# Two graph-attention layers before a transformer layer: preparation placed among products, masks transposed as byte pairs, an order written out by hand

## The chip, the cores and the metric

The kernel runs on one NeuronCore of one Trainium2 chip. The core has five engines that run side by side and wait for each other through semaphores: TensorE (PE; its weight loads are shown as PEld), VectorE (DVE), ScalarE (ACT), GpSimd (POOL) and SyncE (SP), which here issues all DMA transfers from one queue in order. The metric is device time in microseconds (us) of one execution, lower is better.

## The reference

Three layers run one after the other on 4096 rows of 256 features and one 4096 x 4096 adjacency matrix of int32 (0 or 1). The first two are graph-attention layers with 8 heads of 32 features; the third is a transformer layer with masked attention.

```python
def _gat_layer(x, adj_mat, W, a):
    Wh = jnp.einsum('nd,hdo->hno', x, W)
    src = jnp.einsum('hno,ho->hn', Wh, a[:, :O])
    dst = jnp.einsum('hno,ho->hn', Wh, a[:, O:])
    e = jax.nn.leaky_relu(src[:, :, None] + dst[:, None, :], 0.2)
    e = jnp.where(adj_mat[None, :, :] > 0, e, NEG_INF)
    alpha = jax.nn.softmax(e, axis=-1)
    out = jnp.einsum('hnm,hmo->hno', alpha, Wh)
    return jnp.transpose(out, (1, 0, 2)).reshape(N, -1)

h   = elu(_gat_layer(x, adj, W1, a1)) + x
out = elu(_gat_layer(h, adj, W2, a2)) + h
# then: layer norm, masked attention with 8 heads (mask adj != 0), projection,
# layer norm, feed-forward of width 1024 with gelu, both with residuals
```

## The kernel before

**The algebra of a graph layer.** exp(leaky_relu(s + d)) is exp(s) exp(d) where s + d is positive and exp(0.2 s) exp(0.2 d) elsewhere. The kernel never forms the 4096 x 4096 scores. For each head it makes a 0/1 matrix of s >= -d, ANDs it with the mask, and multiplies it (as fp8 stationary operand) with values that have been multiplied with exp(d) and exp(0.2 d) beforehand. The f16 moving operand `vst` holds these values as a high and a low half, with a column for the softmax denominator. The masked sum of the second kind needs the mask itself as stationary operand.

**Blocks, pairs, groups.** A layer's rows are cut into blocks of tiles of 128 rows: layer 1 into 4, 4, 8, 8 and 8 tiles, layer 2 into four times 8 (`TILES`). For each block there are four pairs of heads, and for each pair 8 groups, one for 512 columns of the adjacency (four chunks `m` of 128). A group of eight tiles has 8 x 4 x 4 = 128 products (L1234): for each tile and chunk one of width 132, two of width 66 for the heads, and one of width 132 for the mask. The sums of a pair stand in six PSUM banks; in its last group they are evicted by ACT (L1240, L1246).

**Compare and AND.** `compare` makes the 0/1 matrices of a group two groups ahead: for each chunk and head a DVE comparison (L1023) or an ACT sign (L1021), then one DVE AND with the mask over 2048 int32 words (L1026). There are three such buffers (`t8`). The row terms s come as `s_b`, spread over the partitions by DMA from `s_d` in DRAM.

**Masks.** A mask unit loads 128 x 1024 int32 of the adjacency, clips them on DVE to bf16 (L844), turns eight 128 x 128 squares on PE (L849) and evicts 1024 columns to fp8 on ACT (L850). Block 0 uses its masks from SBUF; every mask is also stored to DRAM (`mask_d`), from where later blocks, layer 2 and the transformer layer fetch them. There are 128 units. Those of blocks 1 to 4 are spread over the groups of the block before.

**Preparation.** For each of 8 parts `q` of 512 rows: `features` transposes the rows (L916, evicted at L919), `term_rows` makes the row terms (L926, L934), and `values` for each of four tiles makes the values by two matmuls (L942), negates the d terms (L950), takes three small exps (L953, L961), the largest value (L954) for a check, scales (L962, L963), casts to the high half on ACT (L971) and subtracts for the low half on DVE (L972). Three of a layer's parts are prepared ahead of its first group, the others one per group beside the first five groups.

**Pair end.** `pair_end` puts four steps on a list, one of which is taken per group: load x, sum (L1053 to L1066), divide and exp (L1073 to L1079), and elu, residual and store (L1085 to L1088).

**Order.** In the graph layers a scheduler puts the instructions of each engine in order from the order of the program and from dependencies. The attention loop of the transformer layer has PE, ACT and DVE in program order (`manual_schedule`). The transformer layer projects q, k and v block by block (L1419, L1440), stores q and k as f16 halves to DRAM (`half_d`) and loads them back stacked (`stack`, L1387), with k's load right after its store; queries and masks of the first attention block are loaded after the last projection. Attention's rows are then projected and pass the feed-forward part (L1628 to L1673).

**Checks.** Conditions under which the fast method holds are gathered in the columns of one tile; if any is not met, `general_layers` computes everything again in a general way.

## Time and profile before

| what | value |
|---|---|
| median of 3 runs | 3524.0 us (3520.53 to 3526.98) |
| profiled execution | 3526.0 us, span 3524.0 us, clock 0.982 |
| PE busy | 3357.4 us (95%) |
| DVE busy | 2903.2 us (82%) |
| ACT busy | 2730.9 us (77%) |
| POOL busy | 1239.1 us (35%) |
| chain that ended last | PE 73%, DVE 11%, ACT 9%, DMA 3%, issue 2%, POOL 2% |
| graph layers | 0 to 1783 us |
| projections of q, k, v | 1796 to 1893 us |
| attention | 1914 to 3227 us |
| output part | 3239 to 3524 us |

The profile is one execution. Its page first gives busy time per engine, then 40 equal slices of the span with the busy share of each engine in tenths, then the chain of work that ended last. Groups of instructions follow, by line, engine and operation, with busy time, mean duration, and the idle time just before them with what ended it. A busy PE isn't a PE at its peak: matmuls are pipelined, and their ends are modelled. Idle time of an engine that isn't on the chain costs nothing.

### The profile page before, as it was taken

How to read it: one execution, taken by the hardware profiler on the slowest of the kernel's cores; microseconds unless marked ns; L12 is line 12 of the kernel's file. 1: busy time of each engine (PE TensorE's matmuls, PEld its weight loads, DVE VectorE, ACT ScalarE, POOL GpSimd, SP SyncE). 2: the span in 40 equal slices, each digit the busy share in tenths (PEclk: the TensorE clock that was granted, in tenths of full speed). 3: DMA queues.
4: the chain of work that ended last, by engine and by line, in shares of the span. 5: the costliest groups of instructions: out<-in, count | busy, mean ns of one | idle time of the engine just before them, and what ended most of it. 6: DMA issues, size and time to landing. Idle time of an engine off the chain costs nothing.

```text
span 3524.0 us, 99099 instructions
## 1 busy us (share of the span) xinstructions
PE 3357.4 (95%) x43715; PEld 2128.8 (60%) x43715; DVE 2903.2 (82%) x3580; ACT 2730.9 (77%) x3528; POOL 1239.1 (35%) x538
## 2 busy tenths in 40 slices
PE   6898999999989999999987999999999999997998
PEld 4698999999969999999963111111111121112666
DVE  5898999999889999999944999999999999996111
ACT  4799999998778888888854777777777777775332
POOL 0000000000000000000001999999999999996110
PEclk8999999999999999999998999999999999998999
DMA  4357554441221312111156010101010110002110
GB/s 140 123 191 242 167 167 157 157 123 39 68 62 33 86 39 80 45 58 37 26 135 171 10 40 13 37 19 31 25 25 25 25 37 13 28 9 68 44 47 25
DMA packets 199560, 252.76 MB, mean 72 GB/s; under 512 B 88080, under 2 KB 134672, under 8 KB 199120
## 3 DMA queue, kind: packets, MB, share of 16 engines
q1 hardware_dynamic: 199120, 246.34, 23.3%
q8 instruction: 344, 5.64, 0.7%
q14 instruction: 96, 0.79, 0.1%
HBM read 203.83 MB, written 42.47 MB: 70 GB/s over the span
## 4 chain that ended last, share of the span: by engine, by line
PE 73%; DVE 11%; ACT 9%; DMA 3%; issue 2%; POOL 2%; SPq 0%; DVEq 0%; ACTq 0%; POOLq 0%
PE bank L1234 34%; PE u_ps L1480 12%; PE u_av L1494 11%; PE u_dn L1494 6%; ACT t L1021 5%; DVE u_e L1489 4%; PE misc L1666 3%; PE misc L1419 2%; POOL u_both L1580 2%; DVE t L1023 1%; ACT u_ps L1487 1%; ACT stage L850 1%; DVE t L1026 1%; PE misc L1650 1%; PE turn L926 1%
## 5 line engine op out<-in xcount | busy, mean ns | idle before, releaser
L1234 PE MATMUL bank<-vst,t 128*128 128x66 f16 (+1 forms) x24576 | 1517.9, 203 | 22.0 <-DVE t L1026 15.5
L1234 PEld LDWEIGHTS <-t 128*128 128x128 fp8e4 x24576 | 1505.6, 97 | 33.2 <-DVE t L1026 18.0
L1234 PE MATMUL bank<-vst,mask 128*128 128x132 f16 x8192 | 1503.5, 222 | 0.0
L1021 ACT ACTIVATE t<-s_b,g_negd 128x1024 int8<-128x1024 f32 (+1 forms) x1296 | 1260.0, 1063 | 88.8 <-PE bank L1234 88.1
L1489 DVE SCALAR_TENSOR_TENSOR u_e<-u_mask,u_ps 128x1024 f32<-128x1024 uint8 x1024 | 1201.7, 1215 | 100.7 <-ACT u_ps L1487 95.8
L1580 POOL TENSOR_TENSOR u_both<-u_e 128x1024 f32<-128x1024 f32 x512 | 1199.8, 2367 | 238.5 <-DVE u_e L1489 238.3
L1487 ACT ACTIVATE u_ps<-u_ps 128x1024 f32<-128x1024 f32 x1024 | 1010.8, 1008 | 296.2 <-PE u_ps L1480 277.2
L1234 PEld LDWEIGHTS <-mask 128*128 128x128 fp8e4 x8192 | 803.6, 98 | 1.9 <-issue 0.9
L1026 DVE TENSOR_TENSOR t<-t,mask 128x2048 int32<-128x2048 int32 (+1 forms) x288 | 590.6, 2051 | 119.5 <-ACT t L1021 109.8
L1023 DVE TENSOR_SCALAR t<-s_b,g_negd 128x1024 fp8e4<-128x1024 f32 (+1 forms) x1008 | 638.5, 687 | 2.7 <-PE bank L1234 2.3
masks.py:197 POOL MEMSET u_ident<- 128x128 f32 x1 | 0.2, 204 | 1785.7 <-DMA u_wq<-in_L_gnn_w_qkv_dram 1785.7
L1480 PE MATMUL u_ps<-u_q,u_k 128*128 128x512 f16 x2048 | 580.5, 384 | 36.8 <-DMA u_q<-half_d 21.7
L1480 PEld LDWEIGHTS <-u_k 128*128 128x128 f16 x2048 | 139.2, 97 | 743.7 <-issue 685.4
L1494 PE MATMUL u_av<-u_e,u_v 128*32 128x512 f32 x4096 | 547.1, 605 | 0.0
L1494 PE MATMUL u_dn<-u_both,u_ones 128*32 128x512 f32 x2048 | 274.0, 605 | 1.3 <-POOL u_both L1580 1.3
L1494 PEld LDWEIGHTS u_av<-u_e,u_v 128*32 128x32 f32 x4096 | 80.9, 108 | 219.1 <-issue 211.3
L1657 ACT ACTIVATE u_hid<-misc,u_b 128x512 f32<-128x512 f32 x64 | 42.3, 683 | 142.9 <-PE misc L1650 142.8
L850 ACT ACTIVATE stage<-turn 128x1024 fp8e4<-128x1024 bf16 x112 | 114.2, 1037 | 1.1 <-PE turn L849 1.0
L1673 DVE TENSOR_TENSOR u_xres<-u_xres,misc 128x256 f32<-128x256 f32 x32 | 13.5, 421 | 122.7 <-PE misc L1666 122.7
L1666 PE MATMUL misc<-u_w,u_hid 128*128 128x256 f32 x512 | 111.8, 379 | 0.0
L1650 PE MATMUL misc<-ln_cols,u_w 128*128 128x512 f32 x256 | 111.2, 592 | 0.0
L1494 PEld LDWEIGHTS u_dn<-u_both,u_ones 128*32 128x32 f32 x2048 | 40.6, 108 | 110.9 <-issue 108.4
(104 smaller groups left out, 1749.8 us busy)
## 6 DMA issues: line engine op xcount, KB each, us to landing
g_rows<-in_adj_dram SPq DMA_DIRECT2D x128, 512.0 KB
mask<-mask SPq DMA_DIRECT2D x120, 256.0 KB
s_b<-s_d SPq DMA_DIRECT2D x56, 512.0 KB
u_mask<-mask SPq DMA_DIRECT2D x32, 512.0 KB
mask<-stage SPq DMA_DIRECT2D x28, 512.0 KB
half_d<-u_halves SPq DMA_DIRECT2D x32, 256.0 KB
u_k<-half_d SPq DMA_DIRECT2D x32, 256.0 KB
u_q<-half_d SPq DMA_DIRECT2D x32, 256.0 KB
```

The costliest lines, as they stand in the source:

```text
L850: nc.scalar.activation(staged[0].rearrange("p i g n -> p (i g) n")[:, :, t * P : (t + 1) * P], pt, AF.Identity, saturate=False,)
L1021: nc.scalar.activation(to.bitcast(I8), s, AF.Sign, bias=negd, scale=-1.0)
L1023: nc.vector.tensor_scalar(to, s, negd, None, op0=ALU.is_ge, saturate=False)
L1026: nc.vector.tensor_tensor(both, both, mask.unsqueeze(1).to_broadcast(list(both.shape)), op=ALU.bitwise_and)
L1234: nc.tensor.matmul(to, left, right, start=k not in opened, stop=last)
L1480: nc.tensor.matmul(ps[:, j, :], k_st[:, h, mt * P : (mt + 1) * P], q_st[:, h, :], start=True, stop=True,)
L1487: nc.scalar.activation(ps, ps, AF.Exp, scale=SCALE)
L1489: nc.vector.scalar_tensor_tensor(e, mask, 0.0, ps, op0=ALU.not_equal, op1=ALU.mult)
L1494: nc.tensor.matmul(to[j * O : (j + 1) * O, :], lefts[j], es[j // 2][:, j % 2, :], start=start, stop=stop,)
L1580: nc.gpsimd.tensor_tensor(both, es_of[i - 1][u], es_of[i][u], op=ALU.add)
L1650: nc.tensor.matmul(ph, w1_sb[:, k, f * P : (f + 1) * P], hn[:, k, :], start=(k == 0), stop=(k == DC - 1),)
L1666: nc.tensor.matmul(po[:, :D], hid[:, f, at : at + P], w2_sb[:, f, :], start=(f == 0), stop=(f == FC - 1),)
```

## The change

All of it lies in the graph layers and in the order of loads around them.

- Layer 1 has four blocks of 8 tiles like layer 2.
- A mask unit is now 256 adjacency rows by 512 columns. Two neighbouring rows are clipped into the two bytes of one 16-bit element (fp8), four 128 x 128 squares of f16 are transposed, and ACT copies 512 16-bit elements. A check sends four bit patterns through such a transpose.
- In `values`, the factor `UP` and the sign of the d terms are folded into the weights; one copy takes both kinds of terms out of PSUM; products are scaled with the exps directly. The cast and the subtraction for the low half become a later step (`split`), and the subtraction goes to POOL. The row terms are transposed from these copies (32 x 128) where two matmuls of 512 columns stood. The three checks on the largest values (`check_values`) are no longer called.
- `manual_schedule` now covers the graph layers: PE, ACT and DVE run in program order. `begin` prepares two parts and eight mask units; the other parts of layer 1 are prepared in groups 0 to 5, those of layer 2 in the last six groups of layer 1 and in groups 3 and 4 of layer 2. Each group has a list of steps with a place between 0 and 1, which are emitted after the tile that they fall on: preparation, compares for two groups on, the AND last, mask units and clips, pair-end steps.
- Pair ends have six steps; the exp has one of its own, two after the division. Sums stand in the eviction tile, the result in the tile of x.
- The next layer's weights reuse one tile and are loaded during block 1.
- In the transformer layer, `k_st` is allocated ahead of `v_sb`, k's stacked loads trail their stores by one block, the first queries and masks are loaded during the projections, and some pools are split; in the output part the projection weights are loaded first.

```diff
-TILES = ((4, 4, 8, 8, 8), (8, 8, 8, 8))
+TILES = ((8, 8, 8, 8), (8, 8, 8, 8))
...
-    mask_p = ctx.enter_context(tc.tile_pool(name="g_mask", bufs=11))
+    mask_p = ctx.enter_context(tc.tile_pool(name="g_mask", bufs=10))
-    rows_p = ctx.enter_context(tc.tile_pool(name="g_rows", bufs=3))
+    rows_p = ctx.enter_context(tc.tile_pool(name="g_rows", bufs=2))
...
+    def mask_load(nb, c, i):
+        r = rows_p.tile([P, 2, G * P], I32, name="g_adj", bufs=3)
+        at = STARTS[0][nb] * P + i * 2 * P
+        nc.sync.dma_start(
+            r,
+            adj[at : at + 2 * P, c * G * P : (c + 1) * G * P].rearrange("(k r) m -> k r m", r=2),
+        )
+        loaded[nb, c, i] = r
...
+    def mask_clip(nb, c, i):
+        v = rows_p.tile([P, G * P, 2], F8, name="adj_8", bufs=6)
+        nc.vector.tensor_scalar(
+            v.rearrange("p m r -> p r m"), loaded.pop((nb, c, i)), 1.0, -(2.0**-30),
+            op0=ALU.min, op1=ALU.max, saturate=False,
+        )
+        clipped[nb, c, i] = v.rearrange("p m r -> p (m r)").bitcast(F16)
+        load_ahead(1)
...
+    def mask_turn(nb, c, i):
+        if i == 0:
+            pool, name = (mask_p, "mask") if nb == 0 else (stage_p, "stage")
+            built[nb, c] = pool.tile([P, NW, G, HB], F8, name=name)
+            if nb == 0:
+                masks.setdefault((0, 0), []).append(built[nb, c])
+        v = clipped.pop((nb, c, i))
+        pt = turn_bank([P, G, P], F16)
+        for m in range(G):
+            nc.tensor.transpose(pt[:, m, :], v[:, m * P : (m + 1) * P], ident_h)
+        to = built[nb, c][:, i // 2].bitcast(U16)
+        nc.scalar.activation(to[:, :, i % 2 * P : (i % 2 + 1) * P], pt.bitcast(U16), AF.Copy)
...
+        def values(t):
+            at = G * q + t
+            pv = bank()
+            for c in range(DC):
+                nc.tensor.matmul(
+                    pv[:, : D + 2 * H],
+                    L.ft[q][:, c, t * P : (t + 1) * P],
+                    L.w_ext[:, c, :],
+                    start=(c == 0),
+                    stop=(c == DC - 1),
+                )
+            nc.vector.tensor_copy(
+                L.terms[:, :, at, :], pv[:, D : D + 2 * H].rearrange("p (k h) -> p k h", k=2)
+            )
+            big = some.tile([P, 2, H], F32, name="g_big")
+            for i, scale in enumerate((-1.0, -LRELU)):
+                nc.scalar.activation(big[:, i, :], L.negd[:, at, :], AF.Exp, scale=scale)
+            nc.scalar.activation(L.r[:, at, :], L.terms[:, 0, at, :], AF.Exp, scale=LRELU - 1.0)
+            nc.vector.tensor_reduce(
+                L.tops[:, at : at + 1], pv[:, :D], AX.X, ALU.max, apply_absolute_value=True
+            )
+            prod = held[t] = some.tile([P, H, 2, V1], F32, name="g_prod")
+            by_head = big.rearrange("p i h -> p h i").unsqueeze(3)
+            nc.vector.tensor_tensor(
+                prod[:, :, :, :O],
+                pv[:, :D].rearrange("p (h o) -> p h o", o=O).unsqueeze(2).to_broadcast([P, H, 2, O]),
+                by_head.to_broadcast([P, H, 2, O]),
+                op=ALU.mult,
+            )
+            nc.vector.tensor_scalar(prod[:, :, :, O:], by_head, UP, None, op0=ALU.mult)
+        def split(t):
+            part = held.pop(t).rearrange("p h i v -> p h (i v)")
+            halves = vst[q][:, t].rearrange("p h (k v) -> p h k v", k=2)
+            nc.scalar.copy(halves[:, :, 0, :], part)
+            nc.gpsimd.tensor_tensor(halves[:, :, 1, :], part, halves[:, :, 0, :], op=ALU.subtract)
+        def term_rows():
+            pr = bank()[: G * H, :P]
+            nc.tensor.transpose(
+                pr, L.terms[:, 0, G * q : G * (q + 1)].rearrange("p t h -> p (t h)"), ident_f
+            )
+            sr = some.tile([G * H, P], F32, name="g_sr")
+            nc.scalar.copy(sr, pr)
+            for t in range(G):
+                at = (G * q + t) * P
+                nc.sync.dma_start(s_d[l][:, at : at + P], sr[t * H : (t + 1) * H])
+        steps = [lambda c=c: features(c) for c in range(DC)]
+        for t in range(G):
+            steps.append(lambda t=t: values(t))
+            if t > 0:
+                steps.append(lambda t=t: split(t - 1))
+        return steps + [term_rows, lambda: split(G - 1)]
...
+        def step_wait():
+            pass
+        def step_exp():
+            nc.scalar.activation(held["ex"], held["z"], AF.Exp)
...
-        later.extend([step_load, step_sum, step_divide, step_out])
+        later.extend([step_load, step_sum, step_divide, step_wait, step_exp, step_out])
...
+    own = [(0, c, k) for c in range(NG) for k in range(2 * NW)]
+    for c in range(2, NG):
+        turns[c - 2] = own[2 * NW * c : 2 * NW * (c + 1)]
     for nb in range(1, len(TILES[0])):
+        units = [(nb, c, k) for c in range(NG) for k in range(2 * NW)]
+        since = max(NG - 2, (nb - 1) * per_block - 4)
+        until = nb * per_block - 4
         for u, unit in enumerate(units):
+            turns.setdefault(since + u * (until - since) // len(units), []).append(unit)
+    coming = own[: 2 * 2 * NW] + [u for i in sorted(turns) for u in turns[i]]
...
+    prepared = {i: (0, i + 2) for i in range(NG - 2)}
+    for l in range(1, NL):
+        start = l * len(TILES[0]) * per_block
+        for q in range(NG):
+            prepared[start + q + (-6 if q < NG - 2 else -3)] = (l, q)
...
+    def begin():
+        rows_ahead(0, 0)
+        weights_of(0)
+        load_ahead(3)
+        units = own[: 2 * 2 * NW]
+        for q in range(2):
+            for k, step in enumerate(preparation(0, q, spare_bank)):
+                step()
+                if q == 1 and k in (2, 4, 6, 8):
+                    mask_clip(*units[k // 2 - 1])
+        s_of[0, 0, 0] = s_fetch(0, 0, 0)
+        for k, u in enumerate(units):
+            mask_turn(*u)
+            if k + 4 < len(units):
+                mask_clip(*units[k + 4])
+            else:
+                mask_clip(*turns[0][k + 4 - len(units)])
+        for i in range(2):
+            for step in compare(i):
+                step()
...
+    ordered = {mybir.EngineType.PE, mybir.EngineType.Activation, mybir.EngineType.DVE}
+    ctx.enter_context(tc.manual_schedule(engines=ordered))
+    begin()
     for i, (l, nb, p, g) in enumerate(groups):
+        if l + 1 < NL and nb == 1 and p == 0 and g == NG - 1:
+            weights_of(l + 1)
+        fetches(i)
+        side = []
+        def beside(steps, since, until):
+            for k, step in enumerate(steps):
+                side.append((since + (until - since) * (k + 0.5) / len(steps), step))
+        made = prepared.get(i)
+        if i + 1 in prepared and prepared[i + 1][0] > 0:
+            if prepared[i + 1][1] in (0, NG - 2):
+                rows_ahead(*prepared[i + 1])
+        if made:
+            steps = preparation(*made, lambda: turn_bank([P, 512], F32))
+            beside(steps, 0.0, 0.9)
+        if i + 2 < len(groups):
+            steps = compare(i + 2)
+            beside(steps[:-1], 0.25 if made else 0.0, 0.95)
+            beside(steps[-1:], 0.96, 1.0)
+        beside([lambda u=u: mask_turn(*u) for u in turns.get(i, ())], 0.0, 0.9)
+        clips = turns.get(i + 2, ()) if i >= NG - 2 else turns.get(i + 1, ())
+        if i == NG - 2:
+            clips = turns.get(i + 1, []) + clips
+        beside([lambda u=u: mask_clip(*u) for u in clips], 0.1, 1.0)
+        beside([take] * (3 if l > 0 and nb == 0 and p == 0 else 1), 0.1, 1.0)
+        side.sort(key=lambda step: step[0])
...
-            if slots:
-                slots.pop(0)()
-        while slots:
-            slots.pop(0)()
+            while side and (n == tiles - 1 or side[0][0] * tiles < n + 1):
+                side.pop(0)[1]()
...
+                for b in (nb - 1,) if nb + 1 < NNB else (nb - 1, nb):
+                    if b >= 0:
+                        at = slice(b * NB, (b + 1) * NB)
+                        stack(k_st[:, :, at], 1, (0, 0, 1, 1), at)
+                    if b == 0:
+                        load_queries(0)
+                if 2 <= nb < 2 + NT // MC:
+                    load_chunk(0, nb - 2)
```

## The prediction

> **What bounds the kernel now.** I read the 40 slices first: PE is nearly full in the graph layers, with soft places at the start, at slice 11 and at slice 20. Then I counted the products (L1234) by stretch:
>
> ```profile
> 0.00:150.00 150.00, 26.80 (x448) 24.85 (x448) 0.90 0.43 132
> 150.00:400.00 250.00, 208.79 (x4280) 203.60 (x4281) 0.97 0.61 198
> 400.00:965.00 565.00, 539.37 (x11660) 534.05 (x11657) 1.00 0.39 122
> 965.00:1067.00 102.00, 36.04 (x706) 34.36 (x706) 0.97 0.19 57
> 1067.00:1784.00 717.00, 716.19 (x15678) 714.40 (x15678) 1.00 0.17 50
> ```
>
> Columns: stretch, its length, PE busy with the count, weight loads, clock, DMA share, GB/s. The first 150 us hold 448 products, the 102 us between the layers 706. The chain of waits, in order of time, gives the price of undisturbed ones:
>
> ```profile
> 637.20 5.82 PE bank L1234 x128
> 643.59 5.82 PE bank L1234 x128
> ...
> 1082.01 46.67 PE bank L1234 x1024
> ```
>
> A group of eight tiles is 8 x 4 x 4 = 128 products. In layer 2 eight groups take 46.67 us, 5.83 each; PE is the bound. In layer 1 the group itself is 5.82, but the next begins 6.39 later: the mask transposes stand between. Both layers hold 256 groups, 1493 us at 5.83; the last product ends at 1783.4. So 290 us of the graph layers are not products: start, masks, preparations. After the layers:
>
> ```profile
> 1783.64 3.47 DMA u_wq<-in_L_gnn_w_qkv_dram
> 1789.99 4.25 DMA u_x<-rows
> 1914.26 2.72 PE L1480 MATMUL u_ps<-u_q,u_k 128*128 128x512 f16 x6 [21.70 <-DMA u_q<-half_d]
> 3239.30 6.11 PE L1628 MATMUL misc<-u_wp,u_att 128*128 128x256 f32 x16 [11.85 <-DMA u_att<-att_d]
> ```
>
> Projection inputs are issued only as the products end (first transpose at 1796.35), attention waits 21.7 us for queries, and the output part 11.9 us for its input. Attention itself (1914 to 3227) is bound by DVE's L1489 and untouched.
>
> Prices, from the groups by form:
>
> ```profile
> L1021 ACT ACTIVATE t<-s_b,g_negd 128x1024 int8<-128x1024 f32 x249 | 267.8, 1168 | 11.3 <-PE bank L1234 11.1
> L1023 DVE TENSOR_SCALAR t<-s_b,g_negd 128x1024 fp8e4<-128x1024 f32 x192 | 131.9, 746 | 0.0
> L1026 DVE TENSOR_TENSOR t<-t,mask 128x2048 int32<-128x2048 int32 x55 | 125.8, 2287 | 25.5 <-ACT t L1021 24.8
> L850 ACT ACTIVATE stage<-turn 128x1024 fp8e4<-128x1024 bf16 x58 | 59.1, 1041 | 0.0
> L844 DVE TENSOR_SCALAR adj_bf<-g_rows 128x1024 bf16<-128x1024 int32 x57 | 38.7, 685 | 0.0
> ```
>
> Neighbours overlap a little: by busy time over count a sign costs 1.07, a compare 0.69, an AND 2.29, a clip 0.68, an eviction 1.02 us.
>
> **What the skill says.** "VectorE: DVE Perf Modes", section "Mode 2×_2P": an operation with one source and both ends in SBUF runs at two elements a cycle if its outermost dimension is even; an fp32 tensor_tensor doesn't. The trace agrees (0.69 us for 1024 elements compared, 2.29 for 2048 ANDed). The new clip has outermost dimension 2, so I keep 0.68; that its two halves write neighbouring bytes no run here shows. "SBUF — State Buffer", section "SBUF: two separate sides": GpSimd and a two-port VectorE operation, or one with two SBUF inputs, lock each other out for a whole instruction. No row of before shows it: POOL's L1580 works beside L1489, which has one SBUF input. "PSUM — Partial Sum Buffer", section "Specifications (TRN2)": a transpose writes its input type uncast; byte pairs in f16 should survive. The trace has only bf16 and f32 transposes.
>
> **The change part by part.**
>
> *Start.* Before, first products at 51 us, but few follow. After, the fixed order has two preparations, eight mask units, and on DVE twelve clips ahead of the first compare. Each clip frees one of three 0.5 MB buffers, and the s_b loads (1 MB) stand between the loads of units 7 and 8 on SP. 12 units, 1 MB of rows, 1 MB of s_b and the weights are some 8.5 MB; at 190 GB/s (slice 4 moved 242, slice 1 140) 45 us. Then five compares 3.4 and an AND 2.3: first product at 53, and the first group's side work starts at 57, when the second group is compared.
>
> *Groups 0 to 5* carry a preparation, four mask units and the compares for two groups on. DVE: 3.5 compares 2.4, AND 2.3, clips 4 x 0.68 = 2.7, values 4 x (0.16 copy + 0.42 maximum + 0.69 product + 0.17) = 5.8; 13.2. ACT: 4.5 signs 4.8, four 512-wide evictions at 0.57 (half of L850's width, near L919's 0.58) 2.3, features 1.2, three small exps and a cast 4 x (0.48 + 0.63) = 4.4, term rows 0.3; 13.0. PE: 5.8 + 3.5 for the preparation + 1; 10.3. The subtractions that left DVE (4 x 0.70) go to POOL at about 1.2 each (half of L1580's 2.37). Under the skill's lock they cost DVE between nothing and 4 x 1.2 = 4.8; I take 2. Sum 15.5 for DVE, x 6 = 93: head ends at 150.
>
> *Groups 6 to 27* have 32 units over 22 groups: PE 5.83 + 1.45 x 4 transposes x 0.06 (0.57 us over 1.18 units of eight, from 6.39 less 5.82) = 6.2; DVE 2.4 + 2.3 + 1.0 + pair end 0.85 (its rows sum to 6.8 for 8 groups) = 6.5, of which rows overlap: in the stretch from 400 DVE was busy 46.3 of 50, which gives 6.1 here. I take 6.25: 137, to 287. *Groups 28 to 91*, one unit each: PE 5.83 + 0.24 = 6.07, ACT 4.8 + 0.57 + 0.6, DVE below 6; 6.08 x 64 = 389, to 676. *Groups 92 to 121*: 30 x 5.83 = 175, to 851.
>
> *Groups 122 to 127* prepare layer 2 beside products: DVE 4.7 + 5.8 = 10.5, ACT 10.7, plus 2 for the lock, less overlap: 12.3. Before, a preparation group's DVE sum was 4.7 + 4 x 2.3 = 13.9, and five of them filled 1000 to 1067, 13.4 each: such sums are reached. 6 x 12.3 = 74, to 925. *Layer 2*: 126 x 5.83 + 2 x 12.3 = 759, to 1684. The rows of parts 6 and 7 need the last pair's store; its six steps, at three a group, end two groups before the load is used, so it hides; if not, 2 to 4 us. The late exp (ACT 0.63 per pair) is moved to a group where its input is long done: the 33 us that L1079 idled cost PE nothing, so nothing. Gain of the graph part: 1783.4 - 1684 = 99.
>
> Why the fixed order need not stall PE: at a pair's end ACT owes 4.5 evictions' worth (0.7 x 6) beside 4 signs, ends some 2.7 us behind PE, and the AND still has a group (5.83) of lead.
>
> *Projections.* u_x and u_wq now stand on SP ahead of layer 2's second half. Then the last pair's sum on DVE (4.8), six squares (0.63 each) and two table loads (1.28 each) on ACT decide: transpose 7 to 8 after the last product instead of 12.9. Gain 5. The 90 us of matmuls stay. *Attention's start*: u_q is loaded from the second projection block on, so only the handover of banks, 1.5 to 2, remains of 21.7: gain 20. *Output*: u_wp first, in space that the scores free 3.4 us earlier; u_att still waits behind u_dens (3231.58): gain 3.
>
> Sum: 99 + 5 + 20 + 3 = 127. The profiled execution took 3526.0 (span 3524.0), the runs' median is 3524.0: 3526 - 127 = 3399, against the median 3397. I say 3398.
>
> **Rivals.** *Half-rate clip*: byte writes to alternate addresses cost one element a cycle, 1.2 us (as L963's 0.69 for 512 suggests). DVE then bounds layer 1: 0.3 x 64 + 0.5 x 22 + 4 x 0.5 x 6 = 42: 3440. For it: nothing like this pattern runs before; against: one-byte outputs of L1023 are not slow. *Cheap head*: no lock and full overlap, 13 a head group and 10.7 a boundary group: 6 x 2.5 + 8 x 1.6 = 28 less: 3370. *Starved head*: DVE, ACT and PE wait for each other in turn, and loads run late, 23 a head group, 14.5 a boundary group: 45 + 18: 3461. Against: before, the sums were met. *Slower*: the fixed order puts the AND last in each group, behind clips and pair steps; if it reaches PE late, every group pays. 256 groups less the 14 with preparations: 0.53 us each (127/242) ends the gain; 0.7 gives 3565. Before, L1026 idled for ACT's signs 119.5 us in all, so the AND is late by nature; but a group of lead stands against it. *Not what it says*: a transposed f16 byte pair fails the new check and the general path runs afterwards, several ms. The PSUM page speaks against it.
>
> **How the numbers follow.** Forecast (3380 to 3418) 50%, half-rate clip 14%, cheap head 15%, starved head 12%, late ANDs 6%, fallback 2%, no change 1%. Range 3352 to 3452 leaves out most of starved, late and fallback, and a tail below. What differs by 0.2% (7 us; the three runs span 6.5) can be told: faster 0.91, same 0.01, slower 0.08.
>
> **What would show it.** Right: last product near 1684, first near 53, head groups at 15 to 16, layer 2 groups still 46.67 for eight, clips near 0.69, u_ps following the projections within 2 us. Wrong: clips over 1 us; PE waiting on the AND in plain groups; POOL's subtractions with DVE gaps of over 1 us; adjacency loads ending PE's or DVE's waits after group 5.

## The result and the profile after

The changed kernel takes 3485.0 us (median of 4 runs, 3482.0 to 3486.8) beside 3524.0 for the kernel before: ratio 0.9889, 95% interval 0.9872 to 0.9906. That is 39 us less where 127 were forecast. The profiled execution's span is 3480.2 us.

The products (now L1302) by stretch, in the same columns as before: stretch, length, PE busy with the count, weight loads, clock, DMA share, GB/s.

```profile
0.00:160.00 160.00, 42.55 (x776) 39.93 (x777) 0.87 0.61 190
160.00:301.00 141.00, 134.14 (x2813) 130.05 (x2810) 1.00 0.64 198
301.00:707.00 406.00, 388.27 (x8196) 378.97 (x8193) 1.00 0.52 157
707.00:884.00 177.00, 176.16 (x3851) 175.25 (x3848) 1.00 0.18 50
884.00:1020.00 136.00, 75.59 (x1409) 72.55 (x1407) 0.96 0.26 82
1020.00:1746.00 726.00, 721.94 (x15747) 717.32 (x15744) 1.00 0.17 51
```

The stretches are cut where groups of 128 products end: 6, 28, 92, 122 and 133 groups. Six groups are done by 160 us (169.7 before), and the last product ends at 1746.2 (1783.6 before). So the graph layers brought 37 us instead of 99: the head (row 1), groups 29 to 92 (row 3), the groups around the layers' boundary (row 5) and layer 2 (row 6, 5.90 us a plain group instead of 5.83) each took longer than forecast.

Then the projections. The timeline of PE of the changed kernel: start, length, line, operation, what it writes and reads, count, and in brackets the idle time before it and what ended it.

```profile
1754.80 2.09 PE L1430 MATMUL misc<-u_ident,ln_rows 128*128 128x128 f32 x8 [8.57 <-DVE ln_rows L1414]
...
1812.29 2.19 PE L1430 MATMUL misc<-u_ident,ln_rows 128*128 128x128 f32 x8 [3.92 <-DVE ln_rows L1414]
...
1830.15 2.15 PE L1430 MATMUL misc<-u_ident,ln_rows 128*128 128x128 f32 x8 [3.92 <-DVE ln_rows L1414]
...
1847.61 2.19 PE L1430 MATMUL misc<-u_ident,ln_rows 128*128 128x128 f32 x8 [3.92 <-DVE ln_rows L1414]
...
1871.74 1.46 PE L1554 MATMUL u_ps<-u_q,u_k 128*128 128x512 f16 x6 [0.46 <-ACT u_v L1528]
3198.92 5.73 PE L1699 MATMUL misc<-u_wp,u_att 128*128 128x256 f32 x16 [12.94 <-DMA u_att<-att_d]
```

The wait for u_q (21.70) has become 0.46, as forecast. But three new waits of 3.92 us stand before the transposes of blocks 5 to 7 (counted from 0), and from one of these to the next 17.5 to 17.9 us pass instead of 11.2 (as from 1785.81 to 1797.01 in this timeline). From the first transpose to the last V product the projections take 116.5 us; before it was 96.2. The three waits are 11.8 of these 20.3 us; the rest is a slower first block (3.2) and transposes and products that take longer after each wait. The 20 us won at attention's start are paid here. The output part still waits for u_att, though from there to the end it takes 281.3 us instead of 284.7.

The groups by form (count, then busy us and mean ns of one, then idle time before and what ended it):

```profile
L1066 ACT ACTIVATE t<-s_b,g_terms 128x1024 int8<-128x1024 f32 x1151 | 1243.6, 1165 | 98.6 <-PE bank L1302 94.7 <-DMA s_b<-s_d 3.8
L1068 DVE TENSOR_SCALAR t<-s_b,g_terms 128x1024 fp8e4<-128x1024 f32 x897 | 636.2, 753 | 0.0
L1073 DVE TENSOR_TENSOR t<-t,mask 128x2048 int32<-128x2048 int32 x256 | 589.8, 2304 | 111.0 <-ACT t L1066 89.6
L864 DVE TENSOR_SCALAR adj<-g_adj 128x1024 fp8e4<-128x1024 int32 x128 | 97.1, 760 | 15.7 <-DMA g_adj<-in_adj_dram 15.7
L1007 POOL TENSOR_TENSOR vst<-g_prod,vst 128x528 f16<-128x528 f32 x64 | 83.9, 1321 | 938.5 <-ACT vst L1006 915.6 <-DVE adj L864 16.6 <-DVE g_prod L1001 6.1
```

The clip costs 0.76 on average, 0.69 where POOL is idle, so writing every second byte costs nothing: the half-rate rival is out. The time of the whole rules out the fallback too.

### The profile page after: what moved, and what is told of

Same layout as the page of the kernel before. It is cut to its first block, busy times and chain, and to the rows that moved or that the text cites. A ratio compares the mean times of both kernels' runs of the same rounds, so it can differ in the third digit from the quotient of the medians.

```text
span 3480.2 us, 97728 instructions
## 1 busy us (share of the span) xinstructions
PE 3297.8 (95%) x43156; PEld 2098.1 (60%) x43156; DVE 2880.6 (83%) x3250; ACT 2655.5 (76%) x3381; POOL 1323.4 (38%) x602
## 4 chain that ended last, share of the span: by engine, by line
PE 39%; DVE 7%; ACT 4%; POOL 2%; issue 1%; DMA 1%; SPq 0%; DVEq 0%; ACTq 0%; POOLq 0%
PE u_ps L1554 12%; PE u_av L1568 11%; PE u_dn L1568 6%; DVE u_e L1563 4%; PE misc L1737 3%; PE bank L1302 2%; POOL u_both L1651 2%; PE misc L1502 2%; ACT u_ps L1561 1%; PE misc L1721 1%; PE misc L1521 1%; ACT ln_square L1406 1%; PE misc L1430 1%; DVE t L1073 1%; ACT t L1066 1%
## 5 line engine op out<-in xcount | busy, mean ns | idle before, releaser
L1302 PE MATMUL bank<-vst,t 128*128 128x66 f16 (+1 forms) x24576 | 1524.2, 203 | 47.5 <-DVE t L1073 39.6
L1302 PEld LDWEIGHTS <-t 128*128 128x128 fp8e4 x24576 | 1506.1, 97 | 66.5 <-DVE t L1073 47.9
L1302 PE MATMUL bank<-vst,mask 128*128 128x132 f16 x8192 | 1506.3, 222 | 0.0
L1066 ACT ACTIVATE t<-s_b,g_terms 128x1024 int8<-128x1024 f32 x1151 | 1243.6, 1165 | 98.6 <-PE bank L1302 94.7
L1563 DVE SCALAR_TENSOR_TENSOR u_e<-u_mask,u_ps 128x1024 f32<-128x1024 uint8 x1024 | 1201.7, 1215 | 89.2 <-ACT u_ps L1561 84.1
L1302 PEld LDWEIGHTS <-mask 128*128 128x128 fp8e4 x8192 | 803.4, 98 | 0.0
L1073 DVE TENSOR_TENSOR t<-t,mask 128x2048 int32<-128x2048 int32 x256 | 589.8, 2304 | 111.0 <-ACT t L1066 89.6
L1068 DVE TENSOR_SCALAR t<-s_b,g_terms 128x1024 fp8e4<-128x1024 f32 x897 | 636.2, 753 | 0.0
L1007 POOL TENSOR_TENSOR vst<-g_prod,vst 128x528 f16<-128x528 f32 x64 | 83.9, 1321 | 938.5 <-ACT vst L1006 915.6
L864 DVE TENSOR_SCALAR adj<-g_adj 128x1024 fp8e4<-128x1024 int32 x128 | 97.1, 760 | 15.7 <-DMA g_adj<-in_adj_dram 15.7
```

The source lines that it names most:

```text
L864: nc.vector.tensor_scalar(v.rearrange("p m r -> p r m"), loaded.pop((nb, c, i)), 1.0, -(2.0**-30), op0=ALU.min, op1=ALU.max, saturate=False,)
L1066: nc.scalar.activation(to.bitcast(I8), s, AF.Sign, bias=negd, scale=-1.0)
L1068: nc.vector.tensor_scalar(to, s, negd, None, op0=ALU.is_ge, saturate=False)
L1073: nc.vector.tensor_tensor(both, both, m32.unsqueeze(1).to_broadcast(list(both.shape)), op=ALU.bitwise_and)
L1302: nc.tensor.matmul(to, left, right, start=k not in opened, stop=last)
L1563: nc.vector.scalar_tensor_tensor(e, mask, 0.0, ps, op0=ALU.not_equal, op1=ALU.mult)
```

## Experiments

All start from the changed kernel. Stage times are read from each run's trace, one execution each. Where an edit doesn't touch a stage, groups 29 to 92 repeat closely (406.0 to 406.1 us in thirteen traces), so this stage shows what a total with a spread of some us can't; projections that no edit touches take 114.8 to 117.2. The head repeats less well: in the changed kernel and the five runs that edit only the projections, the first product comes at 60.3 to 62.4 us and the end of the sixth group at 157.4 to 159.8. A head group is the mean of groups 2 to 6, a boundary group that of groups 123 to 128.

### What made the projections long

`stack_early_2buf`:

```diff
-            hv = qkv.enter_context(tc.tile_pool(name="u_hv", bufs=3))
+            hv = qkv.enter_context(tc.tile_pool(name="u_hv", bufs=2))
...
+                    if i == 1:
+                        stack(k_st[:, :, cols], 1, (0, 0, 1, 1), cols)
...
-                    if b == 0:
-                        load_queries(0)
-                if 2 <= nb < 2 + NT // MC:
-                    load_chunk(0, nb - 2)
...
+        load_queries(0)
+        for k in range(NT // MC):
+            load_chunk(0, k)
```

So k is read back right after its store, and the first queries and masks are loaded behind the projections, both as before the change. `u_hv` holds the f16 halves on their way to DRAM; before the change they had two buffers, the change gave them a third.

> The projections are put back as they were before the change: k is read back from half_d right after its store, queries and mask chunks are loaded after the last block, the halves have two buffers; the graph layers stay changed. My theory: the 20 us that the projections got longer (96.2 us before, 116.8 after, from the first L1430 transpose to the last V product) come from where the layer norms of blocks 5 to 7 stand on DVE. In this version the third of the late norms stands ahead of the last 14 subtractions instead of the last 8, as before the change; so the projections take 96 to 98 us again, the wait for u_q of 21.7 us before the first score comes back, and the whole is unchanged: 3482 to 3488. Rival (transfers: the norms are late because u_x lands late behind other traffic in this place): also 96 to 98, and does not tell the two apart alone; the next run does. Rival (the changed graph part leaves a colder clock or late rows behind): 115 to 118 us and the wait in addition, 3504 to 3508.

Measured: 3475.4 us (ratio 0.9869, 0.9853 to 0.9886). Projections 97.7 us; the first score then waited 7.8 us for u_q, not 21.7, so this is faster than the changed kernel. The graph part isn't to blame.

`stack_early`: the same, with `hv` left at three buffers.

> As the run before, but the halves keep three buffers: SP's order is that of before the change, DVE's order is that of after it. Order on DVE as the cause: the transposes of blocks 5 to 7 wait about 3.9 us each for ln_rows as in the changed kernel, the projections take 115 to 118 us, and the wait for u_q comes back on top: 3503 to 3508. SP's queue as the cause (u_x behind the delayed stacks and chunks): 96 to 98 us, total 3482 to 3488.

Measured: 3490.9 us (0.9916, 0.9899 to 0.9932), projections 114.4 us, the three waits of 3.92 there again, and 11.6 us for u_q. The two runs differ in one number, the buffers of `u_hv`, and with three of them the projections are 16.7 us longer. The moved reads of k and queries alone are not to blame: both are put back here, and it is still slow. How the buffer does it this run does not decide as it was meant to: in its trace u_x stands on SP behind the stores and the reads of k, as in the changed kernel, while with two buffers it came ahead of the reads; the norms stand late on DVE too, so both suspects were present.

`fixed_order`: `manual_schedule` for PE, ACT and DVE around the projections, no line moved.

> The changed kernel with PE, ACT and DVE held to the order of the text in the projections too, so that each block's layer norm stands on DVE ahead of the four subtractions of two blocks earlier; the loads stay where the change put them. Order on DVE as the cause: no wait of 3.9 us before L1430, projections 95 to 99 us, first score within 3 us of the last V product, total 3462 to 3468. If the fixed order makes ACT's squares wait for u_x at the head of each block, some of it is lost again: up to 3475. SP's queue or DMA traffic as the cause: 112 us or more, total 3478 or more.

Measured: 3480.8 us (0.9876, 0.9859 to 0.9893); projections 116.4. DVE's norm now stands ahead of the subtractions, and waits. The waits of this run from 1755 to 1870 us (engine, line, waited for: us in total, times, longest):

```profile
DVE ln_mean L1401 <- DMA u_x<-rows: 26.8, 3, 11.3
...
PE misc L1523 <- ACT ln_cols L1433: 11.3, 3, 5.6
```

My theory falls here, at least as the only cause: with the order on DVE mended, the norm waits for its input.

`turn_first`: the fixed order, with the next block's transposes first and `ready(nb + 2)` between the two halves.

> The changed kernel with the order of PE, ACT and DVE written out in the projections, and in another order than in the run before with a fixed order: the transposes of the next block come first, then half of this block's products, then the layer norm of the block after next. So ACT's two evictions of ln_cols no longer stand behind squares that wait for ln_mean, and DVE's norm stands ahead of the last two subtractions of the block. If the 20 us are the place of the norm on DVE and ACT: no waits of 4 to 5 us before L1430 or in L1523, projections 95 to 99 us, first score within 4 us of the last V product: 3460 to 3468. If a transfer is late (u_x, u_q or a mask chunk in SP's queue): PE waits for ln_rows or u_q remain, 3472 to 3482.

Measured: 3502.2 us (0.9936, 0.9920 to 0.9953), 17 us slower than the changed kernel; DVE waited 24.5 us for u_x and PE 35.1 for ln_rows (12.5 of them at the start). Moving the norm moved its load, too, behind the stores of the first half. The SP timeline of the changed kernel has the same thing:

```profile
1790.93 4.52 SPq L1514 DMA_DIRECT2D half_d<-u_halves  x4
1795.51 1.99 SPq L1455 DMA_DIRECT2D u_k<-half_d  x4
1797.54 0.45 SPq L742 DMA_DIRECT2D u_x<-rows  x1
```

The stores wait for the block's own halves (70.6 us of such waits on SP in this phase), and u_x is issued after them and after four reads of k. In `fixed_order` the same load, issued at 1797.22, ended DVE's wait only at 1806.07, 8.9 us later; in the changed kernel ln_mean began at 1806.18, right behind a subtraction.

`loads_ahead`:

```diff
+            def load_x(nb):
+                if nb < NNB:
+                    landed[nb] = some.tile([P, TB, D], F32, name="u_x", bufs=3)
+                    rows.load(landed[nb], nb * TB)
...
+                load_x(nb + 3)
```

The new call stands ahead of the block's stores; the order is that of `turn_first`.

> As turn_first (fixed order in the projections, transposes of the next block first, the norm of the block after next between the two halves), and u_x is loaded one block earlier into a third buffer, ahead of the block's half_d stores on SP. In turn_first DVE's ln_mean waited 5 to 7 us per block for u_x, issued behind stores that wait for the block's own halves. If the place of the norm and the landing of u_x are all that made the projections long: no wait before L1430 in blocks 2 to 7, projections 95 to 99 us, first score within 4 us of the last V product, 3460 to 3468. If a transfer still comes late in this place (u_x behind the reads of k from half_d): waits of 2 us or more stay, 3470 to 3485.

Measured: 3467.6 us (0.9836, 0.9820 to 0.9853). PE's timeline of this run, from the sixth block on:

```profile
1810.30 1.34 PE L1430 MATMUL misc<-u_ident,ln_rows 128*128 128x128 f32 x8
...
1821.80 1.34 PE L1430 MATMUL misc<-u_ident,ln_rows 128*128 128x128 f32 x8
...
1833.30 1.34 PE L1430 MATMUL misc<-u_ident,ln_rows 128*128 128x128 f32 x8
...
1855.75 1.46 PE L1564 MATMUL u_ps<-u_q,u_k 128*128 128x512 f16 x6 [0.46 <-ACT u_v L1538]
```

A block takes 11.5 us (11.2 before), the projections 101.1, and attention still starts at once. `turn_first` and `loads_ahead` differ in the load of u_x alone, its place and its third buffer: with the norms early, that is worth 133.8 - 101.1 = 32.7 us. But the changed kernel's own trace shows the other suspect at work too. Its DVE never waited for u_x ahead of the three late transposes; for block 6 the load had been issued 15.3 us before the norm began, behind the last of a block's subtractions:

```profile
1808.75 0.45 SPq L742 DMA_DIRECT2D u_x<-rows  x1
1823.44 0.69 DVE L1510 TENSOR_TENSOR u_halves<-misc,u_halves 128x512 f16<-128x512 f32 x1 [1.02 <-ACT u_halves L1509]
1824.05 1.21 DVE L1401 TENSOR_REDUCE ln_mean<-u_x 128x4 f32<-128x1024 f32 x1
```

So the late norms and the late loads come together. Mending the order alone won nothing (`fixed_order`, 116.4), mending both won 15.4 of the 20.3 us, and taking the third buffer of `u_hv` away as well as putting the loads back won 18.8. Neither an earlier load alone nor two buffers of `u_hv` alone were tried on the changed kernel.

### What makes plain groups 5.90 us

The chain of waits of the changed kernel in layer 2 (start, length, what):

```profile
1628.35 19.90 PE bank L1302 x432
1648.27 0.49 ACT ev_broad L1308
...
1654.94 2.77 ACT t L1066 x3
1657.89 1.21 ACT t L1066
1659.13 2.29 DVE t L1073
1661.42 1.33 DVE t L1068 x2
1662.75 1.18 DVE ev_broad L1101
...
1667.05 2.29 DVE t L1073
...
1673.27 2.30 DVE t L1073
1675.62 19.81 PE bank L1302 x432
```

Once in eight groups, 47.27 us apart, the path leaves PE: the evictions of a pair's end push ACT's signs back, the AND waits for them, and the next AND stands behind the pair's sum (L1101 and on); the third releases PE.

`sum_later`:

```diff
- [step_load, step_sum, step_divide, step_wait, step_exp, step_out]
+ [step_load, step_wait, step_sum, step_divide, step_exp, step_out]
```

> A pair's sum and its division come one group later (the empty step moves from behind the division to ahead of the sum). My theory: in plain groups PE is late once in a pair because ACT owes the evictions of the last group, and the AND of the second group after them then stands behind the 3.7 us sum on DVE. With the sum a group later the AND at that place is 3 to 4 us earlier: layer 2's period falls from 47.26 us for eight groups to 46.7, the PE waits on the AND between 301 and 707 us (9.5) fall below 4, and the total falls by 10 to 18: 3467 to 3475. Rival (ACT's evictions alone make the ANDs late): the period stays within 0.1 of 47.26, total 3482 to 3488. Rival (the exp now follows the division by one group and holds ACT up): slower, 3488 to 3496.

Measured: 3479.6 us (0.9876, 0.9860 to 0.9893). Its chain leaves PE later and comes back at

```profile
1674.05 19.81 PE bank L1302 x432
...
1720.84 23.39 PE bank L1302 x511
```

46.79 us apart, and PE waited nowhere for an AND between 1040 and 1740 us. The mechanism holds in layer 2 (720.4 us for the last 123 groups instead of 726.1). The total gained no more than this, 5.4 us: groups 123 to 128 took 86.5 instead of 84.1, and groups 29 to 92 stayed at 406.1, against the expectation.

`four_t8`: t8 with four buffers, the masks with eight.

> A fourth buffer for the compare results t8, so that the signs, compares and ANDs of a group may run a group further ahead of PE; to make room the mask buffers go from ten to eight, and each mask of the next block is fetched one group later. My theory for the plain groups: what each engine must do fits into 5.85 us, and only the burst at a pair's end (ACT's evictions, DVE's 3.7 us sum) makes the AND late once in a pair: layer 2 falls from 47.26 to 46.7 to 46.8 per eight groups (8 us in all). For groups 28 to 91: DVE's steps, counted start to start, need 6.09 us per group and PE's 6.07, so a further buffer takes out the burst's lateness but no more: from 6.34 to 6.10 to 6.20 (9 to 15 us in all). Total 3462 to 3474. Rival (DVE alone is full there): 6.28 to 6.34 stays, total 3476 to 3482. Rival (the masks come late with eight buffers): PE waits on the AND at block starts, no gain or slower, 3484 or more.

Measured: 3485.6 us (0.9889, 0.9872 to 0.9905), the plain groups as before the edit (406.0 in groups 29 to 92, 726.1 in the last 123). Buffers are not what holds the ANDs back; the chain above shows no wait for a released buffer, only instructions in their order.

`four_four`: the comparison goes to ACT for `j == 1` only.

> The compares of a group are split four on ACT and four on DVE; in the changed kernel every second group has five on ACT. That takes 0.53 us per group off ACT and puts 0.33 on DVE. If DVE is what bounds groups 28 to 91 (6.09 us of its own against 6.34 measured): 6.60 to 6.70 there, 422 to 429 us instead of 406.1, total 3505 to 3525. If ACT's lateness after a pair's end bounds them: 6.1 to 6.3, 390 to 404 us, total 3465 to 3480. In layer 2, with no clips, DVE has 5.80 of its own: 47.0 to 47.6 us for eight groups if the DVE sum after the pair's end is what makes PE late there, below 46.9 if it is ACT's evictions.

Measured: 3487.6 us (0.9897, 0.9880 to 0.9913). Groups 29 to 92: 416.1 us, 6.50 each, between both expectations. To read it, DVE's timeline of the changed kernel there:

```profile
536.15 1.41 DVE L1068 TENSOR_SCALAR t<-s_b,g_terms 128x1024 fp8e4<-128x1024 f32 x2
537.47 0.69 DVE L864 TENSOR_SCALAR adj<-g_adj 128x1024 fp8e4<-128x1024 int32 x1
538.07 1.41 DVE L1068 TENSOR_SCALAR t<-s_b,g_terms 128x1024 fp8e4<-128x1024 f32 x2
539.57 2.29 DVE L1073 TENSOR_TENSOR t<-t,mask 128x2048 int32<-128x2048 int32 x1
541.78 1.41 DVE L1068 TENSOR_SCALAR t<-s_b,g_terms 128x1024 fp8e4<-128x1024 f32 x2
```

A group with four compares takes DVE 541.78 - 536.15 = 5.63 us without a gap, one with three 4.99 (506.99 to 511.98); a pair's steps add 3.53 + 1.17 + 1.79, 0.81 a group. So DVE needs (5.63 + 4.99)/2 + 0.81 = 6.12, PE 5.83 + 0.22 for a unit's four transposes (421.81 to 422.03) = 6.05, and 6.34 was measured. The gap is mostly ACT's lateness: in these 64 groups DVE stood idle 11.3 us, 0.18 a group, each time waiting for signs ahead of an AND. In `four_four` DVE needs 5.63 + 0.81 = 6.44 and 6.50 was measured; its waits for signs are 0.9 us in all. DVE is then the bound, and ACT's lateness is gone. In the changed kernel both hold it in turn: DVE's own work, a little more than PE's, and its waits for signs. The same holds in groups 7 to 28, where DVE stood idle 4.8 us in the changed kernel and 0.2 in `four_four`, which took 148.0 us there instead of 141.4. In layer 2 the split four and four gives 5.87 us a group; in the head 15.8, no clear change, since an unedited head shows 16.0 to 16.3.

### What holds the groups with a preparation

PE's waits of the changed kernel, first from 62 to 160 us, then from 884 to 968:

```profile
PE turn L974 <- DVE g_prod L1001: 11.6, 12, 1.2
PE turn L961 <- ACT g_ft L964: 7.5, 6, 2.1
...
PE turn L1012 <- DVE g_terms L981: 7.4, 6, 3.3
PE turn L974 <- ACT g_ft L964: 4.2, 5, 1.7
PE turn L974 <- DVE g_prod L1001: 2.9, 4, 1.5
```

In the six boundary groups PE was busy 69.5 of 84 us, DVE 66.1, ACT 56.2: no engine is full, and PE's 14.5 us of waits are for the two turn banks (PSUM banks for transposes and values) and for the pieces of the others.

`split_on_dve`: L1007 on DVE.

> The second halves of the products (L1007, 64 times) are subtracted on DVE again instead of POOL, all else as changed. My theory: POOL's 1.32 us each holds DVE's large operations up (a clip 0.69 takes 1.65 beside it; 8.4 us of such excess between 60 and 160) and keeps g_prod's buffers longer (15.5 us of waits), which is about what 0.70 on DVE costs; so a head group stays at 15.5 to 17 us and a boundary group at 13.5 to 14.5, and the total moves by less than 8: 3478 to 3492. Rival (the lock is what makes these groups long): head groups at 14 to 15, boundary groups at 12 to 12.5: 3465 to 3475. Rival (DVE's own sum is the bound there): head groups at 18 to 19, boundary groups at 16 to 17: 3502 to 3515.

Measured: 3484.3 us (0.9887, 0.9870 to 0.9903); a head group 16.4 us and a boundary group 14.5. POOL does hold DVE up, as this DVE timeline of the changed kernel shows, with two of POOL's L1007 running from 926.22 to 929.03:

```profile
925.72 2.31 DVE L1068 TENSOR_SCALAR t<-s_b,g_terms 128x1024 fp8e4<-128x1024 f32 x2
928.13 3.04 DVE L1073 TENSOR_TENSOR t<-t,mask 128x2048 int32<-128x2048 int32 x1
```

Elsewhere the two compares take 1.41 and the AND 2.29. It agrees with the Trainium skill's "SBUF — State Buffer", section "SBUF: two separate sides", by which the two lock each other out. But the edit changes two things at once: it takes the lock away and puts 4 x 0.70 us of subtraction on DVE. It shows that the exchange brings nothing, not what the lock alone costs.

`handoffs`: `values` in two steps, `term_rows` last.

> In a group with a preparation, the value step is cut in two (matmuls, terms and exponentials in the first, maximum and product in the next slot), and the rows of terms are transposed last, beside the AND. No work is added or removed. My theory: these groups take 16.2 and 14.0 us against sums of about 12.5 on the busiest engine because PE, DVE and ACT hand four short pieces to each other in a fixed order and each waits for the other: with the pieces apart the waits of ACT's exponentials (26.6 us between 60 and 160, 27.1 between 880 and 990) fall by half or more, PE's wait for g_terms before L1012 (7.4) goes, head groups fall to 14.5 to 15.5, boundary groups to 12.3 to 13.2, total 3468 to 3478. Rival (DVE with POOL's lock is the bound): within 0.4 us per group of 16.2 and 14.0, total 3480 to 3488. Rival (the longer hold of the two turn banks makes PE wait): longer groups, over 3490.

Measured: 3488.5 us (0.9901, 0.9885 to 0.9918); 16.3 and 15.0. In the boundary groups PE's wait for g_terms shrank from 7.4 to 3.1, and 9.2 us of waits for g_sr came before the next group's features: the bank is only passed on later. Nearest to the third outcome.

`exps_from_bank`: the three exps read `pv` instead of `L.terms`.

> In a preparation the three small exponentials read the terms in the PSUM bank instead of the copy that DVE makes of them, so ACT no longer waits for DVE there (26.6 us of such waits between 62 and 160, 27.1 between 884 and 968) and DVE's product no longer waits for ACT. No operation is added or removed. My theory: the head and boundary groups are a chain PE, DVE, ACT, DVE, POOL through two turn banks and two g_prod buffers; with one link less a head group takes 14.5 to 15.5 (16.2), a boundary group 12.5 to 13.3 (14.0), total 3470 to 3480. Rival (DVE's own work and POOL's lock, 13.3 of the 16.2, leave little): 0 to 0.5 per group less, 3481 to 3486. Rival (ACT now stands waiting for PE ahead of its signs): longer, 3488 or more.

Measured: 3488.6 us (0.9899, 0.9883 to 0.9916); 16.3 and 14.1. The link wasn't removed: ACT still waited 29.4 us for DVE's copy (62 to 160), and DVE's maximum now waited 10.2 us for ACT.

`no_maximum`:

```diff
- nc.vector.tensor_reduce(L.tops[:, at : at + 1], pv[:, :D], ..., ALU.max, ...)
```

> The maximum of the values (L989, 0.41 us on DVE, four in a preparation), whose result nothing reads in the changed kernel, is left out. It stands on DVE between the copy of the terms and the product, while ACT makes the exponentials that the product needs. If DVE's own work bounds the groups with a preparation: 4 x 0.33 = 1.3 us less in each, head groups 14.9 (16.2), boundary groups 12.7 (14.0), total 3467 to 3475. If the chain of hand-overs bounds them, DVE waits for ACT's exponentials in that place instead: 0 to 0.4 less per group, 3479 to 3486.

Measured: 3484.0 us (0.9889, 0.9872 to 0.9905); 16.2 and 14.0, unchanged to 0.05. DVE waited for the exps (g_big, 9.1 us from 62 to 160) where the maximum had stood. So DVE's own sum is not the bound here.

`compares_last`: preparation steps over 0 to 0.6 of a group, compares over 0.6 to 0.95.

> In the groups with a preparation, its steps are spread over the first 60 per cent of the group and the signs and compares for two groups on over the last 40, instead of mixed from a quarter on; on the changed kernel, nothing else. If the hand-overs are slow because signs of 1.05 us and compares of 0.66 stand between them on ACT and DVE: the boundary groups fall from 14.0 to 12 to 13 us, head groups from 16.2 to 15 to 15.7, total 3470 to 3480. If the chain of small pieces through two turn banks is slow by itself, the compares now come on top of it: boundary groups 14.5 to 16, total 3490 to 3505.

Measured: 3500.5 us (0.9926, 0.9909 to 0.9942); 18.8 and 15.0. So the compares were not in the way where they stood; it fits that they filled waits.

`clips_after`: the clips for the first group's transposes after the compares of the first group.

> At the start, the four clips of the units that are transposed in the first group come after the compares of the first group instead of ahead of them. My theory: four of the twelve clips that stand on DVE ahead of the first compare wait for adjacency loads (51 to 56 us) behind the s_b loads on SP, though s_b has landed by 47.4; without them the first AND ends some 4 to 7 us earlier, first product at 55 to 59 instead of 62.5, of which most is kept: 3478 to 3483. Rival (the compare waits for s_b and the signs anyway): first product at 61 to 63, total 3482 to 3488. Rival (the head then waits for the late clips, since adjacency loads bound it): first product earlier, end of the sixth group as before at 159 to 161, total unchanged.

Measured: 3480.2 us (0.9876, 0.9859 to 0.9892). First product at 51.6 instead of 62.4, but the first group takes 22 us instead of 16, and six groups are done by 156.6: 3.3 us earlier than in the changed kernel's trace, 0.9 earlier than the earliest of the unedited heads. The head gives most of it back.

### Together

`together`: loads_ahead, clips_after, no_maximum; four and four in the first eight groups; in layer 2 the later sum and five signs in every fourth group.

> What helped, together: the projections as in loads_ahead (17 us less than the changed kernel), the clips as in clips_after (5), the maximum left out (0), four and four compares in the first eight groups (2, as in four_four), and in layer 2 the sum a group later as in sum_later and five compares on ACT only in every fourth group (layer 2's eight groups at 46.7 to 46.8 instead of 47.26, 7 to 8 us). If these lie in different stages and add up: 3451 to 3457. If one hides another, above all the earlier start that the head gives back: 3457 to 3465.

Measured: 3448.1 us (0.9781, 0.9768 to 0.9794), 37 us below the changed kernel and 77 below the one before. Six groups by 152.3, groups 29 to 92 unchanged (406.1), last product 1729.9, first score 1838.8. The 77 us are against the kernel before as it ran beside this one (3525.2). The parts lie in different stages and add up, to a little more than was expected.

## Why the prediction was wrong

The direction was right, the size was not. By its own steps, forecast and measured:

| step | forecast | measured |
|---|---|---|
| first product | 53 | 62.4 |
| from there to the end of group 6 | 97 | 97.4 |
| groups 7 to 28 | 137 (6.25) | 141.4 (6.43) |
| groups 29 to 92 | 389 (6.08) | 406.0 (6.34) |
| groups 93 to 122 | 175 | 176.7 |
| groups 123 to 128 | 74 (12.3) | 84.1 (14.0) |
| layer 2 | 759 | 778.2 |
| last product to first transpose | 7 to 8 | 8.6 |
| projections | 96, unchanged | 116.5 |
| to the first score | 1.5 to 2 | 0.5 |
| wait for u_att | 3 less than 11.85 | 12.94 |
| output part from there | 284.7, unchanged | 281.3 |

By the two traces, with spans of 3524.0 and 3480.2 us, 83 of the 127 us are missing: the projections make 20, groups 7 to 92 make 21, layer 2 makes 19, the groups with a preparation ahead of it 10 and the start 9; the rest is small.

**Projections.** The step that failed worst is "The 90 us of matmuls stay". The queries' reads were put on the gain side alone, and the norms that feed these matmuls were taken to come in time. They do not: 116.5 us instead of 96.2. Nothing was put down for the third buffer of `u_hv` (`stack_early` against `stack_early_2buf`: 114.4 and 97.7 us), nor for u_x, which comes behind stores and reads of k on SP (`turn_first` against `loads_ahead`: 133.8 and 101.1). Why a third buffer leads the scheduler to that order is open.

**Plain groups.** "Why the fixed order need not stall PE" failed: the AND's lead of one group is used up within three groups by a pair's evictions and its sum. It was listed as a rival that ends the gain at 0.53 us per group; in layer 2 it costs 0.07. In groups 29 to 92 "DVE below 6" is the mis-sized term: its prices sum to 6.2 (2.4 + 2.3 + 0.68 + 0.85), an overlap was taken off, and start to start DVE needs 6.12, more than PE; the signs' lateness adds some 0.2. That last part is read from the traces of the changed kernel and of `four_four`; no edit took it away without putting work on DVE.

**Preparations.** Two terms. PE's share of a preparation was taken as 3.5; counted from start to start in the trace of the head it is 4 x 1.05 for L974, 0.93 for L961 and 0.17 for L1012, 5.3. And a group was taken to last as long as its busiest engine; in the boundary groups even PE, the busiest, stands waiting 2.4 us a group for banks and pieces. In the head both are hidden by luck: the DVE sum of 15.5 is close to the measured 16.2, but its parts make 13.2 + 2 = 15.2, and DVE's busy time there is 13.3 a group (66.6 of 81 us in five), with POOL's delays in it. Which link of the chain is the longest is open: five edits moved the waits and none shortened it, and a third turn bank was not tried.

**Start.** 45 us for loads, five compares and an AND gave 53. The twelve clips ahead of the first compare were named as order on DVE, yet the waits of the last four for their loads were not added; `clips_after` shows some 9 to 11 us for them (first product at 51.6 against 60.3 to 62.4), of which 1 to 3 are left by the sixth group.

**Layer 2.** Of its 19 us some 9 are the pair ends (0.07 x 123), the rest groups 129 to 133 (52.1 us in place of 42.1). Groups 129 to 131 prepare nothing and were priced at 5.83; they take 7.8, 8.6 and 7.4, with the evictions and the hurried steps of layer 1's last pair among their signs and compares, 6.2 us in all. The two late preparations take 28.4 in place of 24.6; 2.1 of it is a wait for rows in group 132.

What was right: the clip's price, attention's start, the f16 byte pairs, and the exp, which is not on layer 2's chain.

## What to carry to other kernels

When transfers move on a queue with one order, list what now stands ahead of each, and follow it to who waits for it; the gain at one end of a stage can be paid in its middle. Where a scheduler chooses the order, run a changed buffer count by itself: it can cost more than the loads that it was meant to help. Where three engines need nearly the same time per group, don't take the largest as the group's time: count each from start to start, add the burst that comes once in a period, and see how many groups of lead it uses up. And where short pieces pass between engines and no engine is full, as in the groups with a preparation here, don't expect work taken off one engine to shorten the stage: `no_maximum` took 4 x 0.4 us off DVE and gained nothing.

## What the hardware showed

- Two DVE compares took 2.31 us instead of 1.41, an AND 3.04 instead of 2.29 and a clip 1.65 instead of 0.69 beside POOL subtractions of 1.15 to 1.6 us.
- A PSUM bank that ACT and DVE both only read was used in turns in `exps_from_bank` (from 62 to 160 us ACT waited 29.4 us for DVE's copy, DVE 10.2 for ACT); whether the chip or the semaphores in the program do this, no run tells.
- u_x (0.5 MB) took 0.45 to 0.58 us to issue, and in `fixed_order`, with reads of k issued just ahead of it and behind it, its waiting reader went on 5.8 to 8.9 us after the issue began.
